# Second layer of a graph network: q and k kept on their own channels, attention scores of a head from 32 contraction rows in four rounds, the range guard moved to the sums of exps

## The chip, the cores and the metric

The kernel runs on one core of one Trainium2 chip. The metric is the device time of one launch in microseconds. Before the change it is 1991.55 us, the median of three runs (1985.82 to 1992.9). One further execution was profiled; all times of the trace are counted from its first instruction.

## The reference, cut to what matters

Four graph layers run one after the other on 4096 nodes with 128 features, all over one 4096 x 4096 adjacency matrix; each is `x = layernorm(x + layer(x))`. The change is in the second one, an attention of four heads with 32 channels each, masked by the adjacency:

```python
q = (x @ Wq + bq).reshape(n, H, C)            # H = 4 heads, C = 32 channels
k = (x @ Wk + bk).reshape(n, H, C)
v = (x @ Wv + bv).reshape(n, H, C)
attn = jnp.einsum('nhc,mhc->hnm', q, k) / np.float32(np.sqrt(C))
e = where(adj == 0, 0.0, exp(attn - rowmax))
alpha = e / sum(e)                             # 0 where a row has no neighbour
out = jnp.einsum('hnm,mhc->hnc', alpha, v)
x_r = x @ Ws + bs
beta = jax.nn.sigmoid(jnp.concatenate([out, x_r, out - x_r], axis=-1) @ Wb)
return beta * x_r + (1.0 - beta) * out
```

The third layer multiplies the degree-normalised adjacency (plus identity) by x and by a weight; the fourth is a masked attention whose logits are a sum of one term per row and one per column.

## The kernel before, in words

Nodes are cut into 32 tiles of P = 128 and 8 strips of S = 512. The class `Fast` makes one program in which nothing is subtracted in the exponent; a flag `good` is written on the way, and if it is 0 at the end the whole net is run again by a slower class (`tile_kernel`). In the profiled execution that does not happen.

**Projection (`layer1`, L2202 to L2295).** x is transposed into `XT` (128 channels on the partitions, 4096 nodes along the free axis). For each of 8 strips, and for k and then q, TensorE makes a 128 x 512 product in PSUM (`pqk`, L2255), with channel h*32+c of head h on partition h*32+c. [...] each of q and k is written as a sum of two parts: ScalarE writes the rounded part (L2257), VectorE the rest (L2258), both into a tile `cut` of which five exist. VectorE also takes the largest magnitude for the guard (L2261). `cut` then goes to a DRAM tensor `qk` (L2264, SyncE's queue), and `stack` (L2230, L2233, GpSimd's queue) reads it back so that one head's four combinations lie below each other: partition r*32+c holds part (0,1,0,1)[r] of q in `QS` and part (0,0,1,1)[r] of k in `KS`. A contraction over all 128 partitions of `KS` and `QS` is then (q0+q1)(k0+k1) for one head. V (L2270, L2271) and R = x Ws + bs (L2280, L2281, VectorE adds the bias from PSUM) follow, and a bound on the logits is made from the maxima and written to `good` (L2286 to L2295).

**Attention (`attention_unshifted`, L1986).** The order is written out by hand (`tc.manual_schedule`, L2160 on). There are 8 passes I (strips of rows) with 32 blocks jb (tiles of columns). For a block, `scores` (L2040) makes two PSUM tiles of two heads each, with one 128-row matmul per head (L2045), and after each tile ScalarE takes the exp of 128 x 1024 values (L2052); VectorE then multiplies the 128 x 2048 exps by the mask `at != 0` (L2054). `sums` (L2064) multiplies by V with a column of ones per head (L2071, float32, 64 output columns a head, so that the sum of exps comes out with it). The order on TensorE is scores(n+2), sums(n), scores(n+3), sums(n+1). Three PSUM tiles hold scores, three tiles `e` hold exps. Between these, each fourth block, ScalarE sums half a row tile of the adjacency (`degree`, L2027) and VectorE looks through it (`look`, L2036). `ending` (L2080) closes a pass in small steps that are spread over the next pass. In pass 0, `stack` calls for later strips of k are issued on GpSimd's queue, each behind a small GpSimd copy (`pace`, L2179) that reads an `e` tile; in later passes `stack` fetches the next strip of q into one of the two `QS` buffers.

**What follows (`layers23`).** A ring of 8 adjacency blocks of 1 MB (L2378, SyncE's queue) feeds `convolve` (L2408, L2423); its left operands are the two parts `halves[0]` and `halves[1]` of the scaled features Y, written by `halve` (L2400; ScalarE L2403, VectorE L2404). Block 0 needs both parts. A ring slot is filled again when TensorE and `look` (L2387) have read it.

**Memory.** Pools are laid one behind the other in SBUF, in the order in which they are opened, and closed pools are used again; a new tile waits for the readers of the tiles that lay there. Per partition, behind Y come KS (64 KiB), VA (16.6 KiB), QS (16 KiB), at0 (4 KiB), and then the attention's own small tiles (`ev`, `o`, `sm`, `be`, `rs`, `junk`), the adjacency rows, and the exps. In the layers after it, behind Y come the ring (64 KiB), `halves[0]` and `halves[1]` (16 KiB each). So the ring lies on KS, `halves[0]` on VA, and `halves[1]` on the end of VA and on QS.

Of the kernel before, what the change touches and what calls it, by code (L numbers as in the profile page):

```python
# [9 lines left out]
F32 = mybir.dt.float32  # L10
F32R = mybir.dt.float32r
BF16 = mybir.dt.bfloat16
AF = mybir.ActivationFunctionType
# [13 lines left out]
SAFE = 60.0  # L27
LIMIT = 20.0
# [1628 lines left out]
class Fast(Net):  # L1657
# [328 lines left out]
    def attention_unshifted(self, VA, KS, QS, at0, stack, R, wb):  # L1986
# [4 lines left out]
        with ExitStack() as ctx:  # L1991
# [8 lines left out]
            pace = rot.tile([1, 1], F32, tag="pace", name="pace")  # L2000
# [39 lines left out]
            def scores(I, jb):  # L2040
                e = ep.tile([P, NH, S], F32, tag="e", name="e")
                for h2 in range(0, NH, 2):
                    p = ps_s.tile([P, 2, S], F32, tag="s", name="ps")
                    for h in range(2):
                        nc.tensor.matmul(  # L2045
                            p[:, h, :],
                            lhsT=KS[:, h2 + h, jb * P : (jb + 1) * P],
                            rhs=QS[I % 2][:, h2 + h, :],
                            start=True,
                            stop=True,  # L2050
                        )
                    nc.scalar.activation(e[:, h2 : h2 + 2, :], p, AF.Exp)  # L2052
                at = st["at", I, jb // 4]
                nc.vector.scalar_tensor_tensor(  # L2054
                    e,
                    at[:, jb % 4, :].unsqueeze(1).to_broadcast([P, NH, S]),
                    0.0,
                    e,
                    op0=ALU.not_equal,
                    op1=ALU.mult,  # L2060
                )
                st["e", I, jb] = e
# [17 lines left out]
            def ending(I):  # L2080
# [10 lines left out]
                for a in range(2):  # L2091
                    pt = ps_s.tile([P, 2, S], F32, tag="s", name="pto")[:, 0, :].rearrange("p (b c) -> p b c", b=4)
                    for b in range(4):
                        nc.tensor.transpose(pt[:, b, :], ev[:, a, b * P : (b + 1) * P], self.ident)
                    nc.vector.tensor_scalar(
                        sm[:, a, :, :], pt[:, :, C : C + 65 : 64].rearrange("p b g -> p g b"), 1e-30, None, op0=ALU.max
                    )
                    nc.vector.reciprocal(sm[:, a, :, :], sm[:, a, :, :])
                    yield
                    for b in range(4):  # L2100
                        nc.vector.tensor_tensor(
                            o[:, b, :].rearrange("p (c h) -> p h c", h=NH)[:, 2 * a : 2 * a + 2, :],
                            pt[:, b, :].rearrange("p (g c) -> p g c", g=2)[:, :, 0:C],
                            sm[:, a, :, b].unsqueeze(2).to_broadcast([P, 2, C]),
                            ALU.mult,
                        )
                    yield
# [52 lines left out]
            with tc.manual_schedule():  # L2160
                load(0, 1)
                row(0)
                for n in range(-LEAD, len(seq)):
                    if n + LEAD < len(seq):
# [10 lines left out]
                        if I == 0 and jb % 4 == 0 and jb // 4 + 2 < NS:  # L2175
                            c = jb // 4 + 2
                            if jb:

                                nc.gpsimd.tensor_copy(pace, st["e", I, jb - 1][0:1, 0, 0:1])  # L2179
                            stack(1, KS[:, :, c * S : (c + 1) * S], c)  # L2180
                        if jb == 3 and 0 < I < NS - 1:
                            stack(0, QS[(I + 1) % 2], I + 1)
# [16 lines left out]
                for _ in rest:  # L2199
                    pass  # L2200

    def layer1(self, Wq, bq, Wk, bk, Wv, bv, Ws, bs, Wb, R):  # L2202
# [6 lines left out]
        with ExitStack() as ctx:  # L2209
            self.on_scalar = 4  # L2210
            keep = ctx.enter_context(self.pool(name="keep1", bufs=1))
            KS = keep.tile([P, NH, N], F32R, tag="KS", name="KS")
# [3 lines left out]
            QS = [keep.tile([P, NH, S], F32R, tag=f"QS{k}", name=f"QS{k}") for k in range(2)]  # L2216
# [3 lines left out]
            qk = self.dram.tile([2, 2, P, N], F32, tag="qk", name="qk")  # L2220
# [8 lines left out]

            def stack(a, dst, c):  # L2230

                for r, part in enumerate(((0, 1, 0, 1), (0, 0, 1, 1))[a]):
                    nc.gpsimd.dma_start(  # L2233
                        out=dst[r * C : (r + 1) * C, :, :],
                        in_=qk[a, part, :, c * S : (c + 1) * S].rearrange("(h c) n -> c h n", h=NH),
                    )

            with ExitStack() as pctx:
# [8 lines left out]
                mx = pre.tile([P, 2, NC], F32, tag="mx", name="mx")  # L2247
# [3 lines left out]
                for c in range(NC):  # L2251
                    s = slice(c * S, (c + 1) * S)
                    for a, w, bias in ((1, wk, bkc), (0, wq, bqc)):
                        p = self.ps_t.tile([P, S], F32, tag="pt", name="pqk")
                        nc.tensor.matmul(p, lhsT=w, rhs=XT[:, s], start=True, stop=True)  # L2255
                        cut = rot.tile([P, 2, S], F32R, tag="cut", name="cut", bufs=5)
                        nc.scalar.activation(cut[:, 0, :], p, AF.Identity, bias=bias)  # L2257
                        nc.vector.scalar_tensor_tensor(  # L2258
                            cut[:, 1, :], p, bias, cut[:, 0, :].bitcast(F32), op0=ALU.add, op1=ALU.subtract
                        )  # L2260
                        nc.vector.tensor_reduce(  # L2261
                            mx[:, a, c : c + 1], cut[:, 0, :].bitcast(F32), AX.X, ALU.max, apply_absolute_value=True
                        )
                        nc.sync.dma_start(out=qk[a, :, :, s].rearrange("k p n -> p k n"), in_=cut.bitcast(F32))  # L2264
                        if c < 2:
                            stack(a, (QS[c], KS[:, :, s])[a], c)
# [10 lines left out]
                for g in self.groups():  # L2277
                    p = self.ps_t.tile([P, 4, P], F32, tag="pt", name="pt")
                    for k, t in enumerate(g):
                        nc.tensor.matmul(p[:, k, :], lhsT=XT[:, t * P : (t + 1) * P], rhs=ws, start=True, stop=True)  # L2280
                    nc.vector.tensor_tensor(  # L2281
                        R[:, g[0] : g[-1] + 1, :], p, bsr.unsqueeze(1).to_broadcast([P, 4, D]), ALU.add
                    )

                m2 = pre.tile([P, 2], F32, tag="m2", name="m2")
                nc.vector.tensor_reduce(m2, mx, AX.X, ALU.max)  # L2286
                nc.vector.tensor_tensor(m2[:, 0:1], m2[:, 0:1], m2[:, 1:2], ALU.mult)
                hd = pre.tile([P, NH], F32, tag="hd", name="hd")
                nc.gpsimd.memset(hd, 0.0)
                for h in range(NH):  # L2290
                    nc.gpsimd.memset(hd[h * C : (h + 1) * C, h : h + 1], 1.0)
                p = self.ps_t.tile([P, S], F32, tag="pt", name="pb")
                nc.tensor.matmul(p[0:1, 0:NH], lhsT=m2[:, 0:1], rhs=hd, start=True, stop=True)
                nc.vector.tensor_reduce(m2[0:1, 0:1], p[0:1, 0:NH], AX.X, ALU.max)
                nc.vector.tensor_scalar(self.good[:, 0:1], m2[0:1, 0:1], SAFE, None, op0=ALU.is_le)  # L2295

            self.attention_unshifted(VA, KS, QS, at0, stack, R, wb)
# [330 lines left out]
```

## Time and profile before

| | |
|---|---|
| median of three runs | 1991.55 us |
| the profiled execution | 1991.43 us, of which the span of its trace is 1989.6 us |
| TensorE busy | 1843.4 us (93%), 8408 matmul records |
| VectorE busy | 1737.9 us (87%) |
| ScalarE busy | 1320.4 us (66%) |
| first projection matmul of the second layer (L2255) | at 719.54 us |
| first score matmul (L2045) | at 762.78 us |
| last product with V (L2071) ends | at 1561.68 us |
| DMA, mean over the span | 231 GB/s |

A line of the profile's groups names the source line, the engine, the operation, the tiles written and read, and the number of instructions; behind the bar stand the busy time and the mean time of one, and behind the next bar the idle time of that engine just before them and what ended it. A float32 matmul is recorded as two matmuls; one of F32R as a single one. PEld is the loading of weights, which can run beside a matmul. In a line of the timeline the first number is the start, the second the length of the merged stretch, and the bracket holds the idle time before it. In a line of windows the numbers are the length, the busy time of each engine with its instructions, the granted clock of TensorE, the busy share of the DMA engines and what they moved.

### The profile page before, as it was taken

How to read it: one execution, taken by the hardware profiler on the slowest of the kernel's cores; microseconds unless marked ns; L12 is line 12 of the kernel's file. 1: busy time of each engine (PE TensorE's matmuls, PEld its weight loads, DVE VectorE, ACT ScalarE, POOL GpSimd, SP SyncE). 2: the span in 40 equal slices, each digit the busy share in tenths (PEclk: the TensorE clock that was granted, in tenths of full speed). 3: DMA queues.
4: the chain of work that ended last, by engine and by line, in shares of the span. 5: the costliest groups of instructions: out<-in, count | busy, mean ns of one | idle time of the engine just before them, and what ended most of it. 6: DMA issues, size and time to landing. Idle time of an engine off the chain costs nothing.

```text
span 1989.6 us, 23419 instructions
## 1 busy us (share of the span) xinstructions
PE 1843.4 (93%) x8408; PEld 991.9 (50%) x8423; DVE 1737.9 (87%) x2726; ACT 1320.4 (66%) x1671; POOL 174.2 (9%) x275
## 2 busy tenths in 40 slices
PE   6779999999998688999999999999999899899997
PEld 5347676667667354333333333333333566544443
DVE  6689989998898866789999999999998988878896
ACT  5699999999997744778787877778777422210000
POOL 2311111121100411200000000000000000000000
PEclk9889999999999989999999999999999999999999
DMA  9778989898945876986867676867667799968882
GB/s 322 169 144 152 170 134 173 148 177 147 154 119 171 338 248 225 293 252 212 239 212 233 211 233 212 232 214 235 213 215 249 312 421 421 421 245 317 291 283 77
DMA packets 172719, 459.25 MB, mean 231 GB/s; under 512 B 13372, under 2 KB 56156, under 8 KB 148016
## 3 DMA queue, kind: packets, MB, share of 16 engines
q1 hardware_dynamic: 117408, 339.13, 47.3%
q0 software_dynamic: 45824, 50.88, 20.0%
q10 hardware_dynamic: 9360, 67.64, 10.6%
q8 instruction: 68, 1.11, 0.2%
q14 instruction: 59, 0.48, 0.1%
HBM read 480.59 MB, written 111.23 MB: 297 GB/s over the span
## 4 chain that ended last, share of the span: by engine, by line
PE 43%; DVE 28%; ACT 17%; DMA 7%; issue 5%; SPq 0%; POOL 0%; ACTq 0%; DVEq 0%; POOLq 0%
PE pv L2071 11%; PE pa L1586 10%; DVE e L2054 9%; PE ps L2045 6%; ACT e L2052 4%; DMA ring<-adjf 3%; PE pj L1919 3%; PE pi L1904 3%; DVE nat L2036 2%; ACT w L1837 2%; PE pz L1820 2%; DVE t L1868 2%; ACT s L1860 2%; ACT nat L2027 1%; PE pa L2441 1%
## 5 line engine op out<-in xcount | busy, mean ns | idle before, releaser
L2054 DVE SCALAR_TENSOR_TENSOR e<-at,e 128x2048 f32<-128x2048 bf16 x256 | 582.6, 2286 | 76.0 <-ACT e L2052 75.5
L2052 ACT ACTIVATE e<-ps 128x1024 f32<-128x1024 f32 x512 | 493.2, 1024 | 149.4 <-PE ps L2045 122.0
L2071 PE MATMUL pv<-e,VA 128*64 128x512 f32 x2048 | 498.2, 607 | 6.0 <-DVE e L2054 5.5
L2045 PE MATMUL ps<-QS,KS 128*128 128x512 f32 x1024 | 314.2, 424 | 8.7 <-ACT e L2052 8.1
L2045 PEld LDWEIGHTS ps<-QS,KS 128*128 128x128 f32 x1024 | 170.4, 188 | 235.6 <-ACT e L2052 177.6
L2071 PEld LDWEIGHTS pv<-e,VA 128*64 128x64 f32 x2048 | 125.1, 136 | 250.5 <-issue 215.7
L1586 PE MATMUL pa<-w,Y 128*128 128x512 f32 x448 | 195.6, 594 | 0.0
L1583 DVE SCALAR_TENSOR_TENSOR w<-rho,col,ring 128x512 f32<-128x512 f32 x224 | 163.0, 746 | 25.1 <-PE pa L1586 12.3
L1820 PE MATMUL pz<-HT 128*128 128x512 f32 x288 | 160.0, 638 | 18.8 <-DVE w L1892 9.8
L1904 PE MATMUL pi<-HA,w 128*128 128x129 f32 x1152 | 154.9, 283 | 9.4 <-DVE w L1881 9.4
L1904 PEld LDWEIGHTS pi<-HA,w 128*128 128x128 f32 x1152 | 141.7, 196 | 20.8 <-issue 16.8
L2423 PE MATMUL pa<-ring,Y 128*128 128x512 f32 x512 | 132.3, 409 | 14.5 <-DVE ring L2398 10.0
L1586 PEld LDWEIGHTS pa<-w,Y 128*128 128x128 f32 x448 | 83.6, 190 | 106.4 <-issue 79.2
L2027 ACT ACTIVATE nat<-nat 128x2048 f32<-128x2048 f32 x64 | 122.6, 1915 | 4.9 <-DMA nat<-in_adj_dram 4.9
L1919 PE MATMUL pj<-HA,w 128*128 128x129 f32 x896 | 118.1, 288 | 2.2 <-DVE X L1933 1.1
L2423 PEld LDWEIGHTS pa<-ring,Y 128*128 128x128 f32 x512 | 95.9, 192 | 44.3 <-DVE ring L2398 12.8
L1919 PEld LDWEIGHTS pj<-HA,w 128*128 128x128 f32 x896 | 110.5, 201 | 10.4 <-issue 7.4
L1829 DVE TENSOR_SCALAR t<-pz 128x512 f32<-128x512 f32 x144 | 93.4, 683 | 14.9 <-PE pz L1823 14.9
L1868 DVE SCALAR_TENSOR_TENSOR t<-t,s 128x2048 f32<-128x2048 f32 x36 | 82.3, 2285 | 20.8 <-ACT s L1860 20.8
L1837 ACT ACTIVATE w<-di,dr 128x512 f32<-128x512 f32 x144 | 90.6, 707 | 0.3 <-DMA di<-rows 0.2
L1892 DVE TENSOR_TENSOR w<-w,ptz 128x512 f32<-128x512 f32 x112 | 73.6, 682 | 18.2 <-PE ptz L1887 17.8
L2387 DVE SCALAR_TENSOR_TENSOR odd<-ring 128x1024 bf16<-128x1024 f32 x64 | 78.1, 1220 | 10.0 <-DMA ring<-adjf 9.5
(419 smaller groups left out, 2351.9 us busy)
## 6 DMA issues: line engine op xcount, KB each, us to landing
ring<-adjf SPq DMA_DIRECT2D x128, 1024.0 KB, 13.8
adjf<-in_adj_dram SPq DMA_DIRECT2D x64, 1024.0 KB, 6.8
nat<-in_adj_dram ACTq DMA_DIRECT2D x64, 1024.0 KB, 5.5
ad<-in_adj_dram SPq DMA_DIRECT2D x36, 1024.0 KB, 8.5
adjb<-in_adj_dram POOLq DMA_DIRECT2D x64, 512.0 KB, 11.6
at<-adjb SPq DMA_DIRECT2D x63, 512.0 KB, 3.5
low<-adjb SPq DMA_DIRECT2D x28, 512.0 KB, 5.2
up<-adjb SPq DMA_DIRECT2D x20, 512.0 KB, 6.3
```

The costliest lines, as they stand in the source:

```text
L1583: nc.vector.scalar_tensor_tensor(w, rho[:, I * S : (I + 1) * S], col[:, 0, j : j + 1], at[:, jb, :], op0=ALU.max, op1=ALU.mult)
L1586: nc.tensor.matmul(pa, lhsT=F[:, j, :], rhs=w, start=False, stop=(j == NT - 1), skip_group_check=True)
L1820: nc.tensor.matmul(pz, lhsT=HT[:, j * P : (j + 1) * P], rhs=HT[:, I * S : (I + 1) * S], start=True, stop=False)
L1837: nc.scalar.activation(w[:, jb, :], st[p]["d"][k], AF.Sigmoid, bias=dr[:, 4 * J + jb : 4 * J + jb + 1])
L1904: nc.tensor.matmul(row[I, "po"][ib // 2][:, ib % 2, :], lhsT=st[p]["w0"][:, jb, ib * P : (ib + 1) * P], rhs=HA[:, 4 * J + jb, :], start=False,
L1919: nc.tensor.matmul(pj[:, a, :], lhsT=st[p]["w1"][:, ib, jb * P : (jb + 1) * P], rhs=HA[:, 4 * I + ib, :], start=(ib == 0), stop=(ib == 3),)
L2027: nc.scalar.activation(nat, nat, AF.Identity, accum_out=self.deg2[:, k, i : i + 1])
L2045: nc.tensor.matmul(p[:, h, :], lhsT=KS[:, h2 + h, jb * P : (jb + 1) * P], rhs=QS[I % 2][:, h2 + h, :], start=True, stop=True,)
L2052: nc.scalar.activation(e[:, h2 : h2 + 2, :], p, AF.Exp)
L2054: nc.vector.scalar_tensor_tensor(e, at[:, jb % 4, :].unsqueeze(1).to_broadcast([P, NH, S]), 0.0, e, op0=ALU.not_equal, op1=ALU.mult,)
L2071: nc.tensor.matmul(st["po"][h // 2][g : g + 64, :], lhsT=VA[:, o : o + 64], rhs=e[:, h, :], start=(jb == 0), stop=(jb == NT - 1), skip_gro ...
L2423: nc.tensor.matmul(st["pa"], lhsT=halves[k][:, j, :], rhs=at[:, jb, :], start=(I > 0 and j == k == 0), stop=(j == NT - 1 and k == 1), skip ...
```

## The change

In the projection, the two parts of q and k are written straight into two tiles that stay on chip, `KT` and `QT` (each 128 partitions x 2 parts x 4096, 32 KiB per partition); `cut`, the DRAM tensor `qk`, all `stack` transfers, `pace`, the maxima L2261 and the bound L2286 to L2295 go. A block's scores are made from the 32 partitions of a head: for each of the four combinations of parts there is a round of four matmuls, one per head, each with 32 rows, accumulating in that head's PSUM bank. Both PSUM tiles of a block are taken before the first round, and both exps come after the last. The bias of R is added by GpSimd after a ScalarE copy out of PSUM. The sums of exps of all passes are kept in `dens`, and after the last pass six small instructions (five of VectorE, one TensorE transpose) compare them with 1e-20 and 1e25 and write `good`.

```diff
             def scores(I, jb):
                 e = ep.tile([P, NH, S], F32, tag="e", name="e")
-                for h2 in range(0, NH, 2):
-                    p = ps_s.tile([P, 2, S], F32, tag="s", name="ps")
-                    for h in range(2):
-                        nc.tensor.matmul(
-                            p[:, h, :],
-                            lhsT=KS[:, h2 + h, jb * P : (jb + 1) * P],
-                            rhs=QS[I % 2][:, h2 + h, :],
-                            start=True,
-                            stop=True,
-                        )
-                    nc.scalar.activation(e[:, h2 : h2 + 2, :], p, AF.Exp)
+                ps = [ps_s.tile([P, 2, S], F32, tag="s", name="ps") for _ in range(2)]
+                for k in range(2):
+                    for q in range(2):
+                        for h in range(NH):
+                            r = slice(h * C, (h + 1) * C)
+                            nc.tensor.matmul(
+                                ps[h // 2][:, h % 2, :],
+                                lhsT=KT[r, k, jb * P : (jb + 1) * P],
+                                rhs=QT[r, q, I * S : (I + 1) * S],
+                                start=(k == q == 0),
+                                stop=(k == q == 1),
+                            )
+                for k in range(2):
+                    nc.scalar.activation(e[:, 2 * k : 2 * k + 2, :], ps[k], AF.Exp)
...
                     nc.vector.tensor_scalar(
-                        sm[:, a, :, :], pt[:, :, C : C + 65 : 64].rearrange("p b g -> p g b"), 1e-30, None, op0=ALU.max
-                    )
-                    nc.vector.reciprocal(sm[:, a, :, :], sm[:, a, :, :])
+                        dens[:, I, a, :, :], pt[:, :, C : C + 65 : 64].rearrange("p b g -> p g b"), 1e-30, None, op0=ALU.max
+                    )
+                    nc.vector.reciprocal(sm[:, a, :, :], dens[:, I, a, :, :])
...
-                        if I == 0 and jb % 4 == 0 and jb // 4 + 2 < NS:
-                            c = jb // 4 + 2
-                            if jb:
-
-                                nc.gpsimd.tensor_copy(pace, st["e", I, jb - 1][0:1, 0, 0:1])
-                            stack(1, KS[:, :, c * S : (c + 1) * S], c)
-                        if jb == 3 and 0 < I < NS - 1:
-                            stack(0, QS[(I + 1) % 2], I + 1)
                         scores(I, jb)
...
                 for _ in rest:
                     pass
+                fine = rot.tile([P, 4 * NT + 1], F32, tag="fine", name="fine")
+                den = dens.rearrange("p i a g b -> p (i a g b)")
+                nc.vector.tensor_scalar(fine[:, 0 : 4 * NT], den, LOW, None, op0=ALU.is_ge)
+                nc.vector.scalar_tensor_tensor(
+                    fine[:, 0 : 4 * NT], den, HIGH, fine[:, 0 : 4 * NT], op0=ALU.is_le, op1=ALU.mult,
+                    accum_out=fine[:, 4 * NT :],
+                )
+                nc.vector.tensor_scalar(fine[:, 4 * NT :], fine[:, 4 * NT :], 4.0 * NT, None, op0=ALU.not_equal)
+                p = ps_s.tile([P, 2, S], F32, tag="s", name="pfine")
+                nc.tensor.transpose(p[0:1, 0, 0:P], fine[:, 4 * NT :], self.ident)
+                nc.vector.tensor_reduce(fine[0:1, 0:1], p[0:1, 0, 0:P], AX.X, ALU.max)
+                nc.vector.tensor_scalar(self.good[:, 0:1], fine[0:1, 0:1], 0.5, None, op0=ALU.is_lt)
...
-            KS = keep.tile([P, NH, N], F32R, tag="KS", name="KS")
+            KT = keep.tile([P, 2, N], F32R, tag="KT", name="KT")
+            QT = keep.tile([P, 2, N], F32R, tag="QT", name="QT")
...
-                    for a, w, bias in ((1, wk, bkc), (0, wq, bqc)):
+                    for T, w, bias in ((KT, wk, bkc), (QT, wq, bqc)):
                         p = self.ps_t.tile([P, S], F32, tag="pt", name="pqk")
                         nc.tensor.matmul(p, lhsT=w, rhs=XT[:, s], start=True, stop=True)
-                        cut = rot.tile([P, 2, S], F32R, tag="cut", name="cut", bufs=5)
-                        nc.scalar.activation(cut[:, 0, :], p, AF.Identity, bias=bias)
+                        nc.scalar.activation(T[:, 0, s], p, AF.Identity, bias=bias)
                         nc.vector.scalar_tensor_tensor(
-                            cut[:, 1, :], p, bias, cut[:, 0, :].bitcast(F32), op0=ALU.add, op1=ALU.subtract
+                            T[:, 1, s], p, bias, T[:, 0, s].bitcast(F32), op0=ALU.add, op1=ALU.subtract
                         )
-                        nc.vector.tensor_reduce(
-                            mx[:, a, c : c + 1], cut[:, 0, :].bitcast(F32), AX.X, ALU.max, apply_absolute_value=True
-                        )
-                        nc.sync.dma_start(out=qk[a, :, :, s].rearrange("k p n -> p k n"), in_=cut.bitcast(F32))
-                        if c < 2:
-                            stack(a, (QS[c], KS[:, :, s])[a], c)
...
-                    nc.vector.tensor_tensor(
-                        R[:, g[0] : g[-1] + 1, :], p, bsr.unsqueeze(1).to_broadcast([P, 4, D]), ALU.add
-                    )
+                    r = R[:, g[0] : g[-1] + 1, :]
+                    nc.scalar.copy(r, p)
+                    nc.gpsimd.tensor_tensor(r, r, bsr.unsqueeze(1).to_broadcast([P, 4, D]), ALU.add)
```

The tiles `QS` (16 KiB) go too, so everything behind VA lies 16 KiB nearer to the start: at0, the attention's small tiles (now with `dens` and `fine`) and half of an adjacency row buffer come to lie where `halves[1]` lies later.

## The prediction, made before the changed kernel ran

> **What bounds the kernel now.** I read the page's groups first, then windows by stage, then the timeline of a steady block, of pass 0 and of the two seams. The groups name the pieces of a block:
>
> ```profile
> L2054 DVE SCALAR_TENSOR_TENSOR e<-at,e 128x2048 f32<-128x2048 bf16 x256 | 582.6, 2286 | 76.0 <-ACT e L2052 75.5
> L2052 ACT ACTIVATE e<-ps 128x1024 f32<-128x1024 f32 x512 | 493.2, 1024 | 149.4 <-PE ps L2045 122.0
> L2071 PE MATMUL pv<-e,VA 128*64 128x512 f32 x2048 | 498.2, 607 | 6.0 <-DVE e L2054 5.5
> L2045 PE MATMUL ps<-QS,KS 128*128 128x512 f32 x1024 | 314.2, 424 | 8.7 <-ACT e L2052 8.1
> ```
>
> TensorE waits 15 us in all for the other two, they wait for it: VectorE 76, ScalarE 149. The windows (projection, attention, third layer) say the same:
>
> ```profile
> 719.50:762.80 43.30, 34.54 (x167) 23.52 (x167) 30.93 (x52) 12.45 (x20) 10.90 (x20) 0.88 0.99 323
> 800.00:1561.00 761.00, 751.30 (x3008) 288.49 (x3010) 695.06 (x786) 602.78 (x669) 26.73 (x42) 1.00 0.72 229
> 1592.00:1612.00 20.00, 18.32 (x83) 14.26 (x82) 16.88 (x48) 5.00 (x17) 0.00 (x0) 1.00 1.01 420
> ```
>
> Attention is bound by TensorE (751 of 761 us), the projection by DMA (share 0.99), and the third layer by DMA again (1.01), though TensorE has only 1.7 of 20 us free there. A steady block:
>
> ```profile
> 1201.39 1.20 PE L2045 MATMUL ps<-QS,KS 128*128 128x512 f32 x4
> 1202.52 1.94 PE L2071 MATMUL pv<-e,VA 128*64 128x512 f32 x8
> 1203.98 1.92 ACT L2027 ACTIVATE nat<-nat 128x2048 f32<-128x2048 f32 x1
> 1204.39 1.20 PE L2045 MATMUL ps<-QS,KS 128*128 128x512 f32 x4
> 1205.88 1.94 ACT L2052 ACTIVATE e<-ps 128x1024 f32<-128x1024 f32 x2
> 1207.39 1.20 PE L2045 MATMUL ps<-QS,KS 128*128 128x512 f32 x4
> ```
>
> The reader is to see the pitch of 3.00 us: 1.13 us from scores to the products with V, 1.87 from there to the next scores. The starts inside are: first weights loaded unhidden in 107 ns, then four score matmuls 229 to 237 ns apart, then a gap of some 95 ns before the products; these run as four pairs of 64-column tiles, two starting 7 ns apart, their weight loads too, 429 ns per pair.
>
> **What the Trainium skill says.** "TensorEngine Tiling (Array Packing)", Key Properties: tiles of the array load weights and multiply in parallel, and a change of tiling mode drains the array. The trace agrees for column tiles (7 ns apart) and shows the drain (95 ns at each switch); row tiles it does not have. "TensorE: Matmul & The Clock Gate", Part 3: matmuls in different row groups start some 4 ns apart; four of 32 rows and 512 columns gained 3.07 times. No row of this trace tests that. The same page, LDWEIGHTS: a load takes its columns over 1.2 GHz whatever the rows, so 107 ns for 128; the trace has 107 to 108, and the changed loads have the same 128 columns, so that four of them one behind another (428 ns) would not hide behind a round of 229. "PSUM — Partial Sum Buffer" I need only for banks: the four heads lie in four banks, so concurrent writes don't meet.
>
> **The change part by part**, against the profiled 1991.43 us (span 1989.6 and 1.8 around it), which is 0.1 below the median, so nothing is corrected.
>
> 1. Projection. It lasts from 719.54 to 762.78.
>
> ```profile
>   DMA qk<-cut: 15.2, 7
> L2257 ACT ACTIVATE cut<-pqk,bqc 128x512 fp32r<-128x512 f32 x8 | 5.5, 687 | 11.7 <-DMA qk<-cut 10.6 <-PE pqk L2255 1.0
> L2280 PE MATMUL pt<-ws,XT 128*128 128x128 f32 x64 | 7.4, 277 | 0.0
> ```
>
> The write to DRAM stalls the cut for 15.2 us (7 times, the first line), and TensorE behind it. Without the writes TensorE's work remains: 32 records of pqk at 429 ns = 13.7, V 7.4, R 7.4, together 28.5. VectorE has 16 × 0.75 + 8 × 0.68 = 17.4, ScalarE 16 × 0.69 and eight new copies of 0.58 (like a copy of XT) = 15.7; both fit below 28.5. The GpSimd adds of R are not on the path, as R is wanted at a pass's end. The bound's chain (L2286 to L2295) goes too. First score at 719.5 + 28.5 + 1.3 for the seams = 749.3: **−13.4**, from −15 (no seam) to −9 (the clock, 0.75 around 740, stays low longer).
>
> 2. Pass 0. The GpSimd copies hold `e` tiles, and some exps wait for a whole block:
>
> ```profile
> 785.37 1.94 ACT L2052 ACTIVATE e<-ps 128x1024 f32<-128x1024 f32 x2 [3.41 <-PE pv L2071]
> ```
>
> Four blocks last 3.72 instead of 3.00: 4 × 0.72 = **−2.9** when `pace` goes (0 if the `e` rotation has another cause). The removed `stack` issues of later passes lie on GpSimd's own queue, hidden: 0.
>
> 3. Score rounds. Four heads concurrently, 107 + 3 × 7 to the first full round, four rounds at 229, the gap of 95: 1.14 to 1.17 against 1.13. I take +0.015 a block, 256 × 0.015 = **+4**. Bounds: a gain of 0.06 if the drain between row and column tiles is shorter than between the full array and these (−15), a loss of 0.06 (+15). What lies beyond is a rival, as the mechanism then differs.
>
> 4. Later exps. The first pair of heads is now done with the last: exps begin some 1.25 us behind the first score instead of 0.77. In an ordinary block this hides: exps 1.25 + 1.94 = 3.19, the mask 2.29, ready at 5.5, wanted at 7.1. After `nat` (64 blocks) it doesn't quite: exps till 3.1, `nat` till 5.0, the next block's first exp till 6.0, when the block behind it begins (6.0) and wants that PSUM tile: 64 × 0.05 to 0.1 = 3 to 6. At seven pass ends, where scores of the new pass wait on VectorE already, one or two blocks lose 0.45: 3 to 6. Start of attention, once: 0.5. Of 0 to 14 I take **+7.5**.
>
> 5. Seam to the third layer. All of pass 7's `ending` is among the convolution's first steps:
>
> ```profile
> 1563.46 0.69 DVE L2404 TENSOR_TENSOR Y<-Y,Y 128x512 fp32r<-128x512 f32 x1
> 1565.05 5.69 PE L2423 MATMUL pa<-ring,Y 128*128 128x512 f32 x24
> 1582.50 0.87 DVE L2154 TENSOR_SCALAR Y<-X,deg 128x128 f32<-128x128 f32 x4
> ```
>
> After the change `halves[1]` lies on the small tiles of the attention, so the first L2404 waits for the whole ending and for the new check. The ending alone, its VectorE steps no longer mixed with the convolution's, takes some 14 us from 1562.3; the check (five VectorE steps of 0.15 to 0.3, one transpose, crossings) 1.5; then L2404 0.7: convolution at 1579.5, 14.5 later. Behind the waiting L2404 on VectorE stands every `look` of the ring (L2387); the ninth ring load, issued at 1567.6 before, now goes at about 1581.4. But eight loads are in flight from 1555.2, the eighth lands at 1581.4 (one per 2.485 us), and the ninth took 17 us in the queue. With an empty queue a load took 4.8 us (1555.2 to 1560.0), so DMA, the bound here, is idle for 1.3 to 5 us. TensorE must catch up 14.5 us with 1.2 to 2.4 us free per 20, over the 150 us that follow, and all but makes it. **+5** (1 to 12), the check within.
>
> Sum: −13.4 − 2.9 + 4 + 7.5 + 5 = +0.2, so 1991.6 us. In words: the prologue gains 16, and attention and the seam give it back in small pieces.
>
> **Rivals.** *The pieces stay hidden* (rounds 0, exps 2, seam 2, less 13.4 and 2.9, rounded for a wait of 2 that I can't place): −14, hence 1977. For it: ScalarE has 158 of 761 us free. Against: 3.00 us a block has no gap on TensorE to hide in.
>
> *A round is longer than 229 ns.* It issues eight instructions. The fastest stretch of the trace, bf16, has a load and a matmul every 56 ns; four such are 224 and just hide. At 64 ns a round takes 256, a block 0.116 more, +30, less nothing else: 2021. The skill's 3.07 read as a steady rate gives 4/3.07 × 229 = 298, +0.28 a block, 2063; I hold it for the gain of one group with its start and end. Range 2006 to 2063.
>
> *The other side:* **weight loads of row groups queue.** The mechanism is the load path, the place each round's four loads of 107 ns. It decides as soon as a round's loads exceed 229 ns, that is beyond 57 ns each. Taken one by one, 16 × 107 + 213 + 98 = 2.02 against 1.13 us, 256 × 0.89 = +228, with the rest 2219. For it: row-tile loads don't appear in the trace and the loads are not smaller for 32 rows. Against: the column tiles' loads start 7 ns apart.
>
> *The change doesn't do what it says*, no concurrency at all: 16 × 229 for 4 × 229, +2.75, so 256 × 2.75 = +704, about 2695. Against: the column pairs again.
>
> **How the numbers follow.** About 0.5% (10 us) is what a measurement of this kernel can tell from no change. Chances: forecast 0.40, hidden pieces 0.25, longer round 0.18, queued loads 0.13, none 0.04. The forecast's own range is 1980 to 2002. The range 1970 to 2040 takes in the hidden case and most of the longer rounds; queued loads, none, and 0.03 of the longest rounds stay out, 0.20. Faster is the second case, 0.25; the same 0.40; slower the last three, 0.35.
>
> **What would show it.** 4096 score records of 32 rows in groups of four a few ns apart, rounds near 229 ns; a first score at 749; no 3.7 us blocks in pass 0; blocks of 3.00 to 3.05; exps 1.25 behind the scores; the first L2404 behind L2154 of pass 7, and a DMA gap of 1 to 5 us before the ninth ring load. A load pitch over 57 ns in the rounds, or starts of one round spread by more than some 20 ns, makes the forecast wrong, and so does a block pitch over 3.04 or a seam that TensorE doesn't catch up.

## The result, and the profile after

The changed kernel takes 1985.45 us (median of 20 runs, 1980.52 to 1993.04), the kernel before 1989.82 us (20 runs, 1982.6 to 1996.7) in the same comparison. The ratio is 0.9986, 95% interval 0.9974 to 0.9998: 2.8 us less, between 0.4 and 5.2. (The two medians lie 4.4 us apart; the text goes by the ratio, to which the interval belongs.) The profiled execution took 1988.08 us, with a span of 1986.2.

The groups of the page, after. The score line has four times the records, each with 32 rows:

```profile
L2059 DVE SCALAR_TENSOR_TENSOR e<-at,e 128x2048 f32<-128x2048 bf16 x256 | 583.6, 2287 | 80.2 <-ACT e L2057 79.3
L2057 ACT ACTIVATE e<-ps 128x1024 f32<-128x1024 f32 x512 | 496.2, 1022 | 163.6 <-PE ps L2049 156.8
L2076 PE MATMUL pv<-e,VA 128*64 128x512 f32 x2048 | 498.4, 608 | 2.8 <-DVE e L2059 2.5
L2049 PE MATMUL ps<-QT,KT 32*128 32x512 f32 x4096 | 326.4, 418 | 5.8 <-ACT e L2057 4.6
```

Four times as many score matmuls are busy 326.4 us where 1024 of 128 rows were busy 314.2 (busy time counts overlapping records once). Four row tiles do run side by side. ScalarE now waits 156.8 us for scores instead of 122.0.

The timeline of a steady block, after:

```profile
1194.66 1.22 PE L2049 MATMUL ps<-QT,KT 32*128 32x512 f32 x16
1195.81 1.94 PE L2076 MATMUL pv<-e,VA 128*64 128x512 f32 x8
1195.90 1.94 ACT L2057 ACTIVATE e<-ps 128x1024 f32<-128x1024 f32 x2 [0.35 <-PE ps L2049]
1197.67 1.22 PE L2049 MATMUL ps<-QT,KT 32*128 32x512 f32 x16
```

The pitch is 3.01 us, 1.15 of it from scores to products with V (1.13 before). The exps start 1.24 us behind the first score (0.77 before). The starts of single records, over the 172 steady blocks (under 3.04 us) behind pass 0: the four matmuls of a round start within 4 to 42 ns (two thirds of the rounds within 14), the rounds follow each other after 227 to 236 ns, and the second round 334 to 340 ns behind the first, whose weights nothing hides, as before. The four weight loads of a round start within 4 to 43 ns, while the round before is still streaming.

The windows of the same three stages (projection, attention, third layer), after:

```profile
716.90:746.90 30.00, 29.95 (x182) 21.87 (x183) 18.04 (x25) 17.93 (x29) 6.96 (x6) 1.00 0.03 6
800.00:1552.00 752.00, 746.18 (x5794) 297.15 (x5788) 682.53 (x778) 588.39 (x651) 2.76 (x5) 1.00 0.62 213
1592.00:1612.00 20.00, 20.00 (x93) 15.95 (x93) 18.98 (x52) 5.96 (x20) 0.00 (x0) 1.00 1.01 422
```

The projection is 30.0 us long, with TensorE busy throughout (29.95) and DMA idle (0.03; 0.99 before). In the third layer, TensorE, which came late, now fills 20.00 of 20 us; before it was 18.32.

The idle time ahead of ScalarE's cut of q and k (the waits of its line, time and number): the 15.2 us behind DMA are gone, and only TensorE's own pace is left.

```profile
its engine sat idle before it (us, times) until:
  PE pqk L2254: 2.6, 15
```

The seam to the third layer, in the timeline after. L2150 is among the last steps of pass 7's ending, L2209 is the last step of the check, L2384 writes `halves[1]`, L2403 is the convolution:

```profile
1565.50 0.60 DVE L2150 TENSOR_SCALAR X<-X,mv,rs 128x128 f32<-128x128 f32 x2 [0.24 <-ACT rs L2144]
...
1568.92 0.14 DVE L2209 TENSOR_SCALAR good<-fine 1x1 f32<-1x1 f32 x1
1569.17 1.90 DVE L2384 TENSOR_TENSOR Y<-Y,Y 128x512 fp32r<-128x512 f32 x3
...
1571.47 1.59 PE L2403 MATMUL pa<-ring,Y 128*128 128x512 f32 x3
```

The last product with V ends at 1553.79, so the convolution starts 17.7 us behind it; before it was 3.4. From the fourteenth on, the ring loads land 5.0 to 7.0 us later behind that product than before (three profiles of each kernel), up to the 64th: TensorE catches up until it meets the DMA, and what DMA lost stays.

**The stages, three executions each.** Both kernels were profiled three times, unchanged (the two first profiles and the runs e1, e11, e8, e12). The table is worked out from the starts and ends of records; "seam" runs from the last product with V to the first matmul of the fourth layer, "end" from there to the end of the span, "closing" is the part of it behind the last busy instruction.

| us | before | after | difference of the means |
|---|---|---|---|
| start of the projection | 719.5, 724.0, 717.2 | 717.0, 716.9, 719.4 | −2.4 |
| projection to first score | 43.2, 43.2, 42.2 | 29.9, 30.2, 29.9 | −12.9 |
| attention | 798.9, 798.4, 798.5 | 806.9, 805.8, 805.2 | +7.4 |
| seam and third layer | 166.2, 164.8, 165.2 | 172.2, 172.1, 171.5 | +6.5 |
| end | 261.7, 261.4, 260.9 | 260.2, 257.3, 259.8 | −2.3 |
| of it, closing | 7.2, 7.2, 7.3 | 5.9, 5.9, 5.9 | −1.3 |
| span | 1989.6, 1991.8, 1984.0 | 1986.2, 1982.4, 1985.8 | −3.7 |

Projection, attention, seam and third layer together come to +1.0; the forecast had +0.2. What is faster lies outside them.

### The profile page after: what moved, and what is told of

Same layout as the page of the kernel before. It is cut to its first block, busy times and chain, and to the rows that moved or that the text cites. A ratio compares the mean times of both kernels' runs of the same rounds, so it can differ in the third digit from the quotient of the medians.

```text
span 1986.2 us, 29386 instructions
## 1 busy us (share of the span) xinstructions
PE 1852.3 (93%) x11478; PEld 1011.1 (51%) x11494; DVE 1730.1 (87%) x2704; ACT 1326.8 (67%) x1679; POOL 140.6 (7%) x209
## 4 chain that ended last, share of the span: by engine, by line
PE 49%; DVE 23%; ACT 18%; DMA 5%; issue 4%; SPq 0%; POOL 0%; ACTq 0%; DVEq 0%; POOLq 0%
PE pv L2076 13%; PE pa L1588 10%; PE ps L2049 9%; DVE e L2059 7%; ACT e L2057 4%; ACT w L1839 3%; PE pa L2403 2%; PE pi L1906 2%; PE pj L1921 2%; ACT s L1862 2%; ACT y L1858 2%; PE pz L1822 2%; DVE nat L2038 2%; DMA dj<-rows 2%; ACT y L1854 2%
## 5 line engine op out<-in xcount | busy, mean ns | idle before, releaser
L2057 ACT ACTIVATE e<-ps 128x1024 f32<-128x1024 f32 x512 | 496.2, 1022 | 163.6 <-PE ps L2049 156.8
L2049 PE MATMUL ps<-QT,KT 32*128 32x512 f32 x4096 | 326.4, 418 | 5.8 <-ACT e L2057 4.6
L2049 PEld LDWEIGHTS ps<-QT,KT 32*128 32x128 f32 x4096 | 187.2, 183 | 231.1 <-ACT e L2057 170.4
L1588 PE MATMUL pa<-w,Y 128*128 128x512 f32 x448 | 195.3, 594 | 0.0
L1822 PE MATMUL pz<-HT 128*128 128x512 f32 x288 | 158.6, 633 | 17.8 <-DVE t L1831 7.8
L2403 PE MATMUL pa<-ring,Y 128*128 128x512 f32 x512 | 131.0, 411 | 8.5 <-DVE ring L2378 7.2
L1588 PEld LDWEIGHTS pa<-w,Y 128*128 128x128 f32 x448 | 83.7, 190 | 106.2 <-issue 80.2
L1921 PEld LDWEIGHTS pj<-HA,w 128*128 128x128 f32 x896 | 111.0, 202 | 11.7 <-issue 7.0
L2403 PEld LDWEIGHTS pa<-ring,Y 128*128 128x128 f32 x512 | 97.8, 195 | 34.8 <-DVE ring L2378 9.5
L1879 DVE TENSOR_TENSOR t<-t,y 128x2048 f32<-128x2048 f32 x36 | 82.1, 2282 | 0.9 <-ACT t L1875 0.9
```

What stands on the lines that cost most here:

```text
L1588: nc.tensor.matmul(pa, lhsT=F[:, j, :], rhs=w, start=False, stop=(j == NT - 1), skip_group_check=True)
L1822: nc.tensor.matmul(pz, lhsT=HT[:, j * P : (j + 1) * P], rhs=HT[:, I * S : (I + 1) * S], start=True, stop=False)
L1921: nc.tensor.matmul(pj[:, a, :], lhsT=st[p]["w1"][:, ib, jb * P : (jb + 1) * P], rhs=HA[:, 4 * I + ib, :], start=(ib == 0), stop=(ib == 3),)
L2049: nc.tensor.matmul(ps[h // 2][:, h % 2, :], lhsT=KT[r, k, jb * P : (jb + 1) * P], rhs=QT[r, q, I * S : (I + 1) * S], start=(k == q == 0), ...
L2057: nc.scalar.activation(e[:, 2 * k : 2 * k + 2, :], ps[k], AF.Exp)
L2403: nc.tensor.matmul(st["pa"], lhsT=halves[k][:, j, :], rhs=at[:, jb, :], start=(I > 0 and j == k == 0), stop=(j == NT - 1 and k == 1), skip ...
```

## The experiments

Lengths of stages are from one profiled execution each; ratios are to the kernel before on the same chip. Pass lengths are from the start of a pass's first score to that of the next: in the kernel before 98.4 us (passes 1 to 6), in the changed one 100.0. A block's number counts from the pass's first scores.

**e1, e8, e11, e12: both kernels again.**

> The kernel before, unchanged, profiled once more. If the untouched layers drift from execution to execution: ratio 1.000, and the start of the projection moves by 1 to 3 us against 719.54 while the projection (43.2 us), the attention (798.9 us) and the seam stay within 0.5 us each. If the 2.6 us that the changed kernel gains ahead of its projection come from the change: the start stays at 719.5 within 0.5 us.

> The changed kernel once more, unchanged. If what it gains beyond the stages of the second layer (2.6 us ahead of its projection) is drift: the projection starts somewhere between 717 and 724, as in other executions, while projection (29.9 us), attention (806.5 to 807), the stretch to the last convolution matmul (172) and the closing sequence behind the last busy instruction (5.9 us, 7.2 before) repeat within 0.7 us; ratio 0.997 to 1.001. If the change shortens the first layer: start at 717 within 0.7 us and ratio below 0.998.

> The kernel before, unchanged, one more execution. Stages of the second layer as before: projection 43.2, attention 798 to 799, last product with V to the first matmul of the fourth layer 164 to 166.5 us, closing sequence 7.2 us; start of the projection anywhere from 716 to 724 if the first layer drifts, and above 719 if it is longer in this kernel than in the changed one.

> The changed kernel, unchanged, one more execution. Projection 29.9 to 30.3, attention 806 to 807, last product with V to the first matmul of the fourth layer 172, closing sequence 5.9 us; start of the projection anywhere from 716 to 724 if the first layer drifts, within 0.5 us of 717 if it is shorter in this kernel.

Measured: e1 ratio 0.9994 (0.9981 to 1.0007), e8 ratio 0.9992 (0.9975 to 1.0010); e11 and e12 were run once each, 1985.85 and 1987.61 us, so they have no ratio. The stages of the second layer repeat within 1.7 us, the closing sequence within 0.1. The start of the projection does not: 717.2 to 724.0 for one kernel, 716.9 to 719.4 for the other. Over all fourteen profiles of this study it lies between 717.1 and 724.0 for the six kernels built on the one before and between 710.7 and 723.9 for the eight built on the changed one; their means are 719.9 and 716.4. Code that the change doesn't touch drifts there by more than the effect, so a gain of the first layer is neither shown nor excluded.

**e2 and e5: later exps alone.** The kernel before, with both PSUM tiles taken first:

```diff
-                for h2 in range(0, NH, 2):
-                    p = ps_s.tile([P, 2, S], F32, tag="s", name="ps")
...
+                ps = [ps_s.tile([P, 2, S], F32, tag="s", name="ps") for _ in range(2)]
+                for h in range(NH):              # e5: for h in (0, 2, 3, 1)
...
+                for k in range(2):
+                    nc.scalar.activation(e[:, 2 * k : 2 * k + 2, :], ps[k], AF.Exp)
```

> The kernel before, with stacked q and k and 128-row matmuls, but both PSUM tiles of a block taken ahead of the first matmul and both exps after the last. If the later exps make the changed attention longer: passes 1 to 6 go from 98.4 to 99.7-100 us, attention from 798.9 to about 809 us, the whole +10 us, ratio 1.005. If it is the rounds (weight loads, drain, clock): passes stay at 98.4 to 98.8 us and the ratio at 1.000 to 1.001.

e2 gave passes of 98.4 us and a ratio of 0.9999 (0.9986 to 1.0012). It was no test of lateness: its matmuls stand in the same order, the first tile is complete after two of them, and the exps still start 0.77 us behind the scores. It only shows that taking both tiles together costs nothing in these passes.

> The kernel before with the four 128-row matmuls of a block in the order of heads 0, 2, 3, 1, so that neither PSUM tile is complete ahead of the last matmul and both exps really begin later (about 1.2 us behind the first score instead of 0.77). If the later exps make the changed passes longer: passes 1 to 6 go from 98.4 to about 100 us, attention from 798.9 to about 809, +10 us, ratio 1.005. If it is the rounds: passes stay within 0.3 us of 98.4 and the ratio is 1.000.

The timeline of e5 (still 128-row matmuls):

```profile
1011.10 1.20 PE L2044 MATMUL ps<-QS,KS 128*128 128x512 f32 x4
1012.23 1.94 PE L2071 MATMUL pv<-e,VA 128*64 128x512 f32 x8
1012.34 1.94 ACT L2052 ACTIVATE e<-ps 128x1024 f32<-128x1024 f32 x2 [0.34 <-PE ps L2044]
1014.10 1.20 PE L2044 MATMUL ps<-QS,KS 128*128 128x512 f32 x4
```

Now the exps start 1.24 us behind the first score, as in the changed kernel, with the pitch still 3.00. Passes are 99.46 us, attention is 806.3 instead of 798.6, the ratio 1.0041 (1.0028 to 1.0054). So about 1.1 us of the 1.6 that a changed pass is longer are the later exps. The steady pitch (median of a pass 3.000 before, 3.004 to 3.012 after) adds 32 × 0.009 = 0.3, which is the rounds; 0.2 is left over. Block 6 has it: it takes 3.00 us before and in e5, 3.22 in the changed kernel, in each of passes 1 to 6.

```profile
1062.08 1.94 ACT L2057 ACTIVATE e<-ps 128x1024 f32<-128x1024 f32 x2 [1.80 <-PE ps L2049]
1063.84 1.42 PE L2049 MATMUL ps<-QT,KT 32*128 32x512 f32 x16
```

These 16 matmuls last 1.42 us instead of 1.22. By the starts of their records, those of heads 2 and 3 begin 0.22 to 0.24 us behind those of heads 0 and 1, one round later: their PSUM tile is free only when the second of the two exps has ended (1062.08 + 1.94). Four heads at once want both tiles at once; in e5 the second tile is wanted one matmul later, and the wait doesn't show. The first round is split in this way in blocks 4, 6, 12, 20, 24 and 28 of passes 1 to 6 (0.22 to 0.65 us), and in no other of their blocks; in all 36 cases heads 2 and 3 start 52 to 53 ns behind the end of an exp. Block for block e5 is no copy of the changed kernel (block 2: 3.41 against 3.60, block 12: 3.70 against 3.48); it is the total of a pass that it repeats.

**e4 and e6: the copies of pass 0.**

```diff
e4, the changed kernel:
+                        if I == 0 and jb % 4 == 0 and 0 < jb and jb // 4 + 2 < NS:
+                            nc.gpsimd.tensor_copy(pace, st["e", I, jb - 1][0:1, 0, 0:1])
e6, the kernel before:
-                            if jb:
-                                nc.gpsimd.tensor_copy(pace, st["e", I, jb - 1][0:1, 0, 0:1])
```

> The changed kernel with the five small GpSimd copies of exps put back into pass 0, nothing else. If they caused the 3.7 us blocks: pass 0 goes from 97.4 to about 100.3 us, with four blocks of 3.7 us, +2.9 us on the changed kernel, ratio to before 1.000. If those blocks came from the stacking transfers or the rotation itself: pass 0 stays at 97.4 us.

> The kernel before without the five GpSimd copies of pass 0; the stacking transfers stay and may go earlier. If copy and stacking transfers together cause the 3.7 us blocks (the copy waits behind the issues on GpSimd's queue): the four blocks of 3.72 become 3.00, pass 0 goes from 100.4 to 97.5 us, ratio 0.9985. If the early exps cause them and the copies matter little: at least three of the four blocks stay at 3.7 us.

e4: pass 0 stays short, 97.7 us, with no block of 3.7; ratio 0.9992 (0.9977 to 1.0007). The copies alone do not do it. e6: pass 0 falls from 100.3 to 97.6 us, all four blocks are 3.00; the ratio is 0.9972 (0.9961 to 0.9984), that is 5.6 us, of which pass 0 is 2.8; the rest is not accounted for. Copies and stacking transfers together do it, and the exps in the timeline of e6 no longer wait for a product with V; the idle time ahead of each is the usual wait for its scores:

```profile
782.24 1.94 ACT L2052 ACTIVATE e<-ps 128x1024 f32<-128x1024 f32 x2 [1.06 <-PE ps L2045]
...
785.24 1.94 ACT L2052 ACTIVATE e<-ps 128x1024 f32<-128x1024 f32 x2 [1.06 <-PE ps L2045]
```

How they do it stands in the programs: the blocks of the kernel before take their `e` buffers (numbered by their addresses) in the order 0 2 1 0 2 1 **2 1** 0 2 **0** 1 2 ..., those of e4, e6 and the changed kernel in the order 0 2 1 0 2 1 0 2 1 throughout. A block that gets the buffer of two blocks before must wait for that block's products with V, which end just before: block 6, with buffer 2 of block 4, is the exp at 785.37 that waited 3.41 us, and these products end at 785.32. The copies themselves are not what differs: they take the same times in e4 (176 to 2209 ns, 177 to 2177 before), and nothing waits for them. The order of the buffers slips only where copies and stacking transfers are both in the program; why is not shown.

**e3: the layout.**

```diff
+            keep.tile([P, 2, NH, S], F32, tag="pad", name="pad")
             at0 = keep.tile([P, 4, S], BF16, tag="at0", name="at0")
```

> The changed kernel with 16 KiB of unused space where QS lay, so that the second part of the scaled features no longer lies on the small tiles of the attention. If the layout makes the seam longer: the convolution starts about 3.5 us after the last product with V instead of 17.7, the stretch from that product to the last convolution matmul goes from 172.4 back to about 167 us, 5 us less than the changed kernel, ratio to before about 0.996. If the DMA there hides the late start: the stretch stays above 171 us and the time within 1 us of the changed kernel.

The timeline of e3; the convolution (L2404) no longer waits, and the check (L2200 to L2209) comes behind it:

```profile
1558.77 5.70 PE L2404 MATMUL pa<-ring,Y 128*128 128x512 f32 x24
...
1574.23 0.23 DVE L2200 TENSOR_SCALAR fine<-dens 128x128 f32<-128x128 f32 x1
...
1575.76 0.14 DVE L2209 TENSOR_SCALAR good<-fine 1x1 f32<-1x1 f32 x1
```

It starts 3.2 us behind the last product with V. The stretch to the last convolution matmul is 167.9 us, the seam of the table 168.3 against 171.9; ratio 0.9966 (0.9948 to 0.9984). The overlap costs 3.6 us. 2.9 us against the kernel before remain. The ninth ring load goes out 5.8 us behind the last product with V (5.9 before, 21.4 in the changed kernel), but the twelfth 25.6 behind it (17.9 before), when the check and the rest of the ending stand in VectorE's queue. The trace shows the wait: two `look`s in a row (L2368) lie 12 us apart, with the ending, the check and the start of the third layer's weights between them, and SyncE, which issues the ring loads (L2359), waits up to 11.7 us for them.

```profile
1566.88 1.21 DVE L2368 SCALAR_TENSOR_TENSOR odd<-ring 128x1024 bf16<-128x1024 f32 x1
...
1578.93 1.22 DVE L2368 SCALAR_TENSOR_TENSOR odd<-ring 128x1024 bf16<-128x1024 f32 x1
```

```profile
SPq L2359 <- DVE odd L2368: 33.8, 9, 11.7
```

Up to the eleventh, the ring loads land 0.2 to 3.2 us earlier behind the last product with V than before; from the fourteenth to the 64th, 2.1 to 3.3 us later. So the remainder is DMA time too, lost behind the twelfth load; no run moved the check to try it.

**e7 and e10: the wait of the exps, and a faster kernel.** e7 is e3 with one more `yield` ahead of each of two ScalarE groups of the ending (the exp of beta; the logarithms and exps of the row statistics). e10 is e7 with the 1.92 us of `degree` cut in two, the second half one block later:

```diff
e7:
                 yield
+                yield
                 nc.scalar.activation(be[:, 0, :], be[:, 0, :], AF.Exp, scale=-1.0)
...
                 yield
+                yield
                 nc.scalar.activation(rs, rs, AF.Ln)
e10:
-                nc.scalar.activation(nat, nat, AF.Identity, accum_out=self.deg2[:, k, i : i + 1])
+                v = nat[:, 0 : N // 4]
+                nc.scalar.activation(v, v, AF.Identity, accum_out=self.deg2[:, k, i : i + 1])
...
+                v = nat[:, N // 4 : N // 2]
+                nc.scalar.activation(v, v, AF.Identity, accum_out=deg3[:, k, i : i + 1])
```

> The changed kernel with the 16 KiB of unused space where QS lay, and with the two ScalarE groups of a pass's ending (the exp of beta, and the logarithms and exps of the row statistics) one block later. If ScalarE's waits for VectorE there cost the passes their time, with exps that begin later: blocks 12 and 24 go from about 3.47 and 3.63 to 3.0-3.2, passes from 100.0 to about 99.1 us, attention 6 us shorter, ratio to before about 0.994. If VectorE's steps themselves are the cause: the two blocks only move by one or shrink by under 0.2 us, and the time is that of the kernel with the space alone, ratio 0.9966.

> The kernel with the space and the two later ScalarE groups, and each sum over half a row tile cut into two of 0.96 us that stand in two consecutive blocks. If the 1.92 us that ScalarE spends on it ahead of the exps is what makes blocks 12, 20 and 28 late (3.47, 3.45, 3.33): they go to 3.0-3.2, passes from 99.2 to about 98.2 us, attention from 799.8 to about 792, ratio to before about 0.990. If VectorE's steps there are the cause: those blocks stay within 0.15 us and passes above 98.9 us.

| | passes 1 to 6, us | block 2 | 4 | 6 | 12 | 20 | 24 | 28 | attention | ratio |
|---|---|---|---|---|---|---|---|---|---|---|
| before | 98.4 | 3.41 | 3.61 | 3.00 | 3.22 | 3.29 | 3.18 | 3.74 | 798.9 | 1 |
| after | 100.0 | 3.60 | 3.91 | 3.22 | 3.48 | 3.68 | 3.62 | 3.31 | 806.9 | 0.9986 |
| e7 | 99.2 | 3.60 | 3.94 | 3.22 | 3.46 | 3.46 | 3.02 | 3.33 | 799.8 | 0.9934 (0.9909 to 0.9958) |
| e10 | 98.75 | 3.60 | 3.82 | 3.23 | 3.19 | 3.14 | 3.01 | 3.63 | 803.8 | 0.9938 (0.9921 to 0.9956) |

The lengths of blocks are medians over passes 1 to 6.

ScalarE's waits over passes 1 to 6 (time, times, longest), in the changed kernel:

```profile
ACT rs L2143 <- DVE rs L2139: 6.0, 6, 1.0
...
ACT be L2125 <- DVE be L2123: 2.1, 6, 0.5
```

In e7 neither line is left. Block 24 is cured by that; block 12 is not, though its wait is gone too, so there the expectation failed. e10 points to its cause: exps that begin late because `nat` stands ahead of them. Cutting it brings blocks 12 and 20 down to 3.19 and 3.14, as expected, but makes 28 longer, so that a pass takes 98.75 us and not 98.2, and blocks 2, 4 and 6 stay. In pass 7 (112.9 us, 107.1 in e7) e10 loses what it gained: the rows are asked for a block later, and ScalarE waits 2.65 us for one in block 18, which takes 9.29 us. Both beat the two kernels; by ratio they can't be told apart. (The short span of e7's profile, 1969.3, is in part a first layer that ended 6 us early.)

**e9: the writes without the rotation.** The changed kernel, which writes its parts to a DRAM tensor that nobody reads:

```diff
+                        nc.sync.dma_start(
+                            out=qk[0 if T is QT else 1, :, :, s].rearrange("k p n -> p k n"), in_=T[:, :, s].bitcast(F32)
+                        )
```

> The changed kernel with the 16 writes of the parts of q and k to a DRAM tensor put back on SyncE's queue, which nobody reads; the parts stay in their own tiles, so no buffer waits for a write. If it was the short rotation of the buffers that made the projection long: it stays at 30 to 31 us, and the attention at 806.5. If DMA itself slows the projection: 35 us or more. If the closing sequence is 1.3 us shorter because SyncE's program is shorter: it goes from 5.9 back towards 7.2 us; if that is due to something else of the change, it stays at 5.9.

The window of its projection:

```profile
711.80:741.80 30.00, 30.00 (x186) 21.87 (x186) 18.05 (x25) 17.93 (x29) 6.99 (x6) 1.00 0.79 285
```

DMA moves 285 GB/s and the projection is still 30.0 us, TensorE busy all of it. So the writes by themselves cost nothing. That the five `cut` tiles waited for them is the 15.2 us of the profile before; how much of that wait came from the reads by `stack`, which shared the DMA and are not in this kernel, is not separated. The closing sequence is 6.1 us, so the length of SyncE's program is not what shortens it. Ratio 0.9983 (0.9972 to 0.9994).

## Why the prediction failed, step by step

The forecast was 1991.6 us and no change that can be measured; measured is a ratio of 0.9986, a little faster. The mechanism that it named as likeliest is what happened in the main; the sum, +0.2, should have been about −0.6 without the first and fourth layers, and something below that if these gain.

1. **Projection: −13.4, measured −12.9** (−13.3 in the first pair of profiles). The step holds: TensorE's own work is all that is left (28.5 + 1.3 = 29.8 was the sum, 29.9 to 30.2 measured), and e9 shows that writing alone does not stall it.
2. **Pass 0: −2.9, measured −2.8 (e6).** The size was right, the reason in part wrong. The prediction had the copies hold the tiles; e4 has the copies and no long block. It is the slipped order of buffers. That the number came out is luck in part: the copies' going does bring it, but not because they held a tile.
3. **Rounds: +4, measured +2.3** (256 × 0.009; the forecast had 0.015 a block). Four loads of 32 rows do start within 4 to 43 ns and hide behind the round before. The sharpest doubt, the price of 107 ns a load in the Trainium skill's "TensorE: Matmul & The Clock Gate", LDWEIGHTS, was not in the load itself but in whether four of them share the time. (The trace gives 107 only between starts: in the kernel before, the second load of a block starts 107 ns behind the first matmul; in the changed one, those of the second round start 106 to 107 behind it; the records of the loads last 181 to 203 ns.) "TensorEngine Tiling (Array Packing)", Key Properties, is right in this trace: row tiles load and multiply in parallel. The 3.07 of Part 3 of the former page isn't what a stream of rounds reaches: 16 matmuls take 1.15 us from first score to products with V where four of 128 rows took 1.13. The rivals of queued loads, of no concurrency and of longer rounds fall with this: matmuls of 128 rows were 229 to 238 ns apart, rounds are 227 to 236. One sign of being wrong was set too sharply: in a fifth of the rounds of steady blocks the starts spread by more than 20 ns, up to 42, and the rounds are no longer for it. That concurrent heads must lie in different banks was not tried; no run puts two into one.
4. **Later exps: +7.5, measured +7.9** (attention +7.4, less the −2.8 of pass 0 and the +2.3 of the rounds); e5 has +7.7 in the kernel before. The size holds, the place only in part. The forecast had 0.05 to 0.1 us in each of 64 blocks behind `nat`; but three of the eight blocks behind `nat` in a pass (0, 8 and 16) stay within 0.03 us of the pitch. All the loss sits in blocks 2, 4, 6, 12, 20 and 24 of a pass, 0.2 to 0.4 us each, and block 28 gives 0.4 back; in e7, moving steps of the ending took the loss of block 24 away. What blocks 4, 6, 12, 20 and 24 wait for is what the forecast named, a PSUM tile that a late exp still holds (block 6 of e5's paragraph). So the size is luck in part.
5. **Seam: +5, measured +6.5.** The convolution starts 17.7 us behind the last product with V (forecast 1579.5 − 1561.7 = 17.8), the ninth ring load 21.4 behind it (19.7), 3.3 us after the eighth has landed (a DMA gap of 1.3 to 5 was forecast). The agreement of the start is partly a slip: the forecast's own terms, 1562.3 + 14 + 1.5 + 0.7, give 1578.5. TensorE catches up, DMA doesn't. The layout is 3.6 of it (e3); by the trace of e3, the other 2.9 follow from the late twelfth load.

Sum of these as measured: +1.0, where +0.2 was forecast and −2.8 is measured. **The step that failed** is the last one, "Sum: −13.4 − 2.9 + 4 + 7.5 + 5 = +0.2, so 1991.6 us": it put everything outside the edited parts at nothing, without a reason. It wasn't nothing. Behind the last busy instruction the kernel before needs 7.1 to 7.3 us in all six of its profiles, the changed one 5.9 to 6.1 in all eight: −1.3. In all six profiles of the former, SyncE pauses 1.2 to 1.3 us between two waits of its closing list (in the first from 1986.98 to 1988.21), and in the changed kernel's it doesn't. Another −0.3 lies between the last matmul of the fourth layer's sums (L1586, now L1588) and the last busy instruction (6.24 and 5.96 in every profile). With these the sum is −0.6, inside the measured interval of −5.2 to −0.4 but 2.2 us short of its middle.

What makes SyncE pause is open. e9 excludes the number of its transfers in the projection; not tried are GpSimd's stacking transfers, which all six kernels with the pause have and none of the others, and a wait for SyncE's own instructions. Whether the first and fourth layers add to the gain is open as well. The first has −2.4 between means of three, with a spread of 7 us within one kernel. But in all seven comparisons of kernels with the change the ratio gains more, by 1.3 to 6.9 us, than the stages named here do in the profile of that kernel; for the four built on the kernel before it is between 0.7 less and 4.9 more. So −0.6 is probably not all.

The forecast also took 10 us, 0.5%, for the least that can be told from no change. With twenty runs of each kernel the interval is 0.12% to either side. Even so the gain is at the edge of what is shown: the interval ends 0.4 us short of no change, and that of the repetition e8 (0.9975 to 1.0010) includes it.

The rival of hidden pieces, at 1977, is wrong although the time lies on its side: nothing was hidden, the pieces cost 8 and 6.5 us. It is what e7 comes near to, once they are removed by hand.

## What to carry to other kernels

Four matmuls of 32 rows side by side took a stream of rounds almost no longer than one of 128 rows each (0.009 us more in a block of 3.00), so a layout need not be stacked for TensorE's sake; what it costs is that all heads are done at the same time: they want all their PSUM tiles at once, and the engine that follows starts later. Ask of such a change which blocks have no slack for that: those where the next engines also have other work, not those of the steady pitch. And look at where a removed tile moves its neighbours in memory: here 16 KiB less put small tiles under a buffer of the next stage, and 16 KiB of nothing gave 3.6 us of it back.

## What was not expected of the hardware and the program

A program's closing sequence is not a constant: 7.2 us before, 5.9 after, each within 0.1 us over three executions; the difference is one pause of 1.2 us on SyncE, whose cause is open. And a stage that no edit touches can drift by more than the effect looked for: the first layer ended between 716.9 and 724.0 us in six executions of the two unchanged kernels, while the attention repeated within 1.7 us. A difference of 0.1% is better read from the stages than from one execution of the whole.
